# Scores of four node tiles as one level of Strassen's scheme, in a fused graph and attention kernel

## The chip, the cores and the metric

The kernel runs on one core of a Trainium2 chip. The metric is the device time of one execution in microseconds (us); three runs of the kernel before gave a median of 2294.43 us (2293.65 to 2296.58).

The core's engines work in parallel, each on its own queue of instructions and in the order of that queue: TensorE (PE: matmuls, from SBUF into PSUM), VectorE (DVE), ScalarE (ACT), GpSimd (POOL) and SyncE (SP, which here only starts transfers). They wait for one another through semaphores.

## The reference

Inputs are 625 nodes of width 512 with 10,000 edges and the weights of four layers. `x` passes through four residual steps, each on a layer norm of `x`: a hyperbolic graph convolution, a feed-forward step with 8 experts, a plain graph convolution, and an attention over 100 pooled memory slots. Only the last one is touched here. Cut to what matters:

```python
G, H, DQK, DV, L = 8, 16, 128, 128, 100           # 8 groups of 16 heads, 100 slots
q  = (xn @ Wq_w + Wq_b).reshape(b, s, G, H, DQK)   # 625 nodes, 128 heads
kc = einsum('bsd,bsl->bld', k, w).reshape(b, L, G, DQK)   # pooled keys
vc = einsum('bsd,bsl->bld', v, w).reshape(b, L, G, DV)    # pooled values
qk = einsum('bsghd,blgd->bghsl', q, kc) * (1.0 / DQK ** 0.5)
att = softmax(qk, axis=-1)
z  = einsum('bghsl,blgd->bsghd', att, vc).reshape(b, s, G * H * DV)
zn = l2norm(z) * wz_g1
h1 = silu(zn @ wz_w1 + wz_b1)                      # 16384 -> 1024
out = silu((l2norm(h1) * wz_g2) @ wz_w2 + wz_b2)
```

All of it is float32.

## The kernel before

The 625 nodes are five tiles of 125 rows (`P`, `NT`). The attention walks over 32 blocks of four heads (`HB`, `NB`). A block `b` passes through these stages:

- `load(b)` starts the transfers on SyncE's queue: 512 rows of `wz_w1` (2 MB, `wz`), the four heads' columns of `Wq_w` in 16 pieces of 64 KB (`wqraw`), and the bias of the scores, spread over the rows (`cb`). The columns are stored so that 32x32 block transposes complete their turning.
- `turned(b)`: four VectorE transposes, 128x512, from `wqraw` into `wqT` (L1101).
- `folded(b)`: 16 matmuls (`kbps`, L1110) multiply the queries' weights into the pooled keys, so that the queries are never formed; ScalarE copies the result into `keys` (128 x 4 chunks x 400 columns).
- `scores(b)`: for each node tile four matmuls of 400 columns over the four chunks of 128 (`scps`, L1123). VectorE adds the bias while it takes the result out of PSUM (L1124) and finds the maxima (L1126). ScalarE takes exponentials, 20 of 100 columns (L1131), then scales them (L1142).
- `transposes(b, h)` turns a head's attention on TensorE; `value(b, h)` multiplies it with the pooled values (`zps`, L1159). ScalarE squares the result into `zs`, one buffer (L1162), VectorE scales it into `zT` (L1163), and GpSimd adds the squares up in `zsq` (L1166).
- `prepared(b)` forms the sums that two levels of Strassen's scheme need for h1 = z w: `zsums` makes eight sums of values on VectorE (L1173 to L1176), `wsums` four sums of weights on VectorE (`wsum`, and `wz` in place; L1182), and `split` four more on GpSimd for each of the seven outer products (`wq`, eight buffers).
- `hidden(b)`: 98 matmuls of 157 columns (`h1ps`, L1222), gathered six to a PSUM buffer; VectorE adds each buffer into `hacc` (L1234).

PSUM holds four buffers of two banks, which all these stages share in turn (`banks`). `h1ps` of block i-2 is issued at the head of iteration i of the loop (L1239 to L1263); the scores of block i close it, so that TensorE goes from scores straight into `h1ps` of the block before, whose sums `zsums` has just made. Instructions of one engine are placed by a scheduler, which may move them where nothing forbids it; `order(later, sooner)` fixes two of them. `busy` issues matmuls that keep TensorE occupied while it would wait.

Of the kernel before, what the change touches and what calls it, by code (L numbers as in the profile page):

```python
# [28 lines left out]
DC = D // 128  # L29
# [9 lines left out]

QN = 157  # L40

ORDER = (0, 1, 2, 5, 3, 4, 6)


HALF = 375
# [6 lines left out]
AHEAD = 12  # L52

HOT = 8

HB = 4

# [110 lines left out]
def layers_kernel(  # L168
# [885 lines left out]
    with ExitStack() as es:  # L1054
# [14 lines left out]
        zq = [big.tile([128, 7, QN], F32, name=f"zq{i}") for i in range(3)]  # L1069

        NB = G * H // HB
        wz, raw, wqT, keys, cb, att, zquarter, whalf, ready = {}, {}, {}, {}, {}, {}, {}, {}, {}
        heads = ExitStack()
        work = spool(heads, "atwork", 2)
        ps_heads = ExitStack()
# [5 lines left out]
        def load(b):  # L1081


            wz[b] = stream.tile([128, HB, FF2], F32, tag="wz", name="wz", bufs=2)
            nc.sync.dma_start(wz[b], wz_w1[b * HB * DH : (b + 1) * HB * DH, :].rearrange("(c p) m -> p c m", p=128))
            cols = Wq_w[:, b * HB * DH : (b + 1) * HB * DH].rearrange("(i a) (h j b) -> j a h i b", a=32, b=32, j=4)
            raw[b] = []
            for h in range(HB):
                raw[b].append(stream.tile([128, D], F32, tag="raw", name="wqraw", bufs=4))
                to = raw[b][h].rearrange("p (i b) -> p i b", b=32)  # L1090
                for j in range(4):
                    nc.sync.dma_start(to[32 * j : 32 * (j + 1)], cols[j, :, h])
            cb[b] = work.tile([P, HB * L], F32, tag="cb", name="cb", bufs=1)
            nc.sync.dma_start(cb[b], bass.AP(tensor=qbias.tensor, offset=qbias.offset + b * HB * L,
                                             ap=[[0, P], [1, HB * L]]))

        def turned(b):
            wqT[b] = []
            for part in raw[b]:
                wqT[b].append(stream.tile([128, D], F32, tag="wqT", name="wqT", bufs=4))  # L1100
                V.transpose(wqT[b][-1], part)  # L1101

        def folded(b):

            keys[b] = work.tile([128, DC * HB * L], F32, tag="keys", name="keys", bufs=1).rearrange("p (c n) -> p c n", c=DC)
            for c in range(0, DC, 2):
# [4 lines left out]
                                 kcT[:, b * HB // H, :], start=True, stop=True)  # L1111
                A.activation(keys[b][:, c : c + 2, :], ps[:, :, : HB * L], AF.Copy, scale=float(DH) ** -0.5)

        def scores(b):
            s = att[b] = work.tile([128, NT * HB * L], F32, tag="att", name="att", bufs=1)[:P].rearrange("p (t n) -> p t n", t=NT)
            top = rpool.tile([P, NT, HB], F32, tag="a_top", name="a_top")
            tot = rpool.tile([P, NT, HB], F32, tag="a_tot", name="a_tot")
            for t0 in range(0, NT, 2):
                t1 = min(t0 + 2, NT)
                ps = banks("scps")  # L1120
                for t in range(t0, t1):
                    for c in range(DC):
                        T.matmul(ps[:P, t - t0, : HB * L], xnT[:, c, tp(t)], keys[b][:, c, :], start=c == 0, stop=c == DC - 1)  # L1123
                V.tensor_tensor(s[:, t0:t1, :], ps[:P, : t1 - t0, : HB * L],  # L1124
                                cb[b][:, None, :].to_broadcast([P, t1 - t0, HB * L]), op=OP.add)
                V.tensor_reduce(top[:, t0:t1, :].rearrange("p t h -> p (t h)"),  # L1126
                                s[:, t0:t1, :].rearrange("p t (h l) -> p (t h) l", l=L), axis=AX.X, op=OP.max, negate=True)
                for t in range(t0, t1):
                    for h in range(HB):
                        own = s[:, t, h * L : (h + 1) * L]  # L1130
                        A.activation(own, own, AF.Exp, bias=top[:, t, h : h + 1], accum_out=tot[:, t, h : h + 1])  # L1131
            V.reciprocal(tot, tot)  # L1132
            if b == 0:

                sv = s.rearrange("p t (h l) -> p (t h) l", l=L)
                V.tensor_tensor(sv, sv, tot.rearrange("p t h -> p (t h)")[:, :, None].to_broadcast([P, NT * HB, L]),
                                op=OP.mult)
                return
            for t in range(NT):
                for h in range(HB):  # L1140
                    own = s[:, t, h * L : (h + 1) * L]
                    A.activation(own, own, AF.Copy, scale=tot[:, t, h : h + 1])  # L1142
# [12 lines left out]
        def value(b, h):  # L1155
            g = b * HB // H
            ps = banks("zps")
            for u in range(2):
# [3 lines left out]
            A.activation(zs, ps[:, :, : 2 * QN], AF.Square)  # L1162
            scaled = V.tensor_scalar(zT[:, h % 2 : 4 : 2, h // 2, :], ps[:, :, : 2 * QN], g1T[:, b * HB + h : b * HB + h + 1],  # L1163
                                     None, op0=OP.mult)
            if b < NB - 1:
                nc.gpsimd.tensor_tensor(zsq, zsq, zs.rearrange("p u s -> p (u s)"), op=OP.add)  # L1166
                return scaled
            return V.tensor_tensor(zsq, zsq, zs.rearrange("p u s -> p (u s)"), op=OP.add)

        def zsums(z, to):  # L1170


            V.tensor_tensor(to[0], z[1][0], z[1][1], op=OP.add)  # L1173
            V.tensor_tensor(to[1], to[0], z[0][0], op=OP.subtract)
            V.tensor_tensor(to[2], z[0][1], to[1], op=OP.subtract)
            V.tensor_tensor(z[1][0], z[0][0], z[1][0], op=OP.subtract)  # L1176
            return {0: z[0][0], 1: z[0][1], 2: to[2], 5: to[1], 3: z[1][1], 4: to[0], 6: z[1][0]}

        def wsums(engine, w, new, over):

            def combine(x, y, to):
                engine.tensor_tensor(to, x, y, op=OP.subtract)  # L1182
                return to
            t1 = combine(w[0][1], w[0][0], new())
            t2 = combine(w[1][1], t1, new())
# [9 lines left out]
        def prepared(b):  # L1195


            zsums([[zT[:, 2 * u + k] for k in range(2)] for u in range(2)], [zT[:, 4 + i] for i in range(3)])
            z = zT.rearrange("p i k (u s) -> p i k u s", u=2)
            zquarter[b] = zsums([[z[:, :, k, u] for k in range(2)] for u in range(2)], zq)  # L1200
            w = wz[b].rearrange("p (q k) (v m) -> p k v q m", k=2, v=2)
            whalf[b] = wsums(V, [[w[:, k, v] for v in range(2)] for k in range(2)],
                             lambda: work.tile([128, 2, FF2 // 2], F32, tag="wsum", name="wsum", bufs=3), True)
            ready[b] = split(b, ORDER[0])


# [2 lines left out]
        def hidden(b):  # L1209
# [3 lines left out]
            for n, i in enumerate(ORDER):  # L1213
# [3 lines left out]
                for j in ORDER:  # L1217
                    for m in range(2):
# [6 lines left out]
                        if at % 6 == 0 or at == 98:  # L1225
# [3 lines left out]
                            else:  # L1229
                                to = to.rearrange("p (k i) s -> p k (i s)", k=2)  # L1230
                            if b == 0:
                                V.tensor_copy(to, got)
                            else:
                                V.tensor_tensor(to, to, got, op=OP.add)  # L1234


        load(0)
# [1 line left out]
        for i in range(NB + 1):  # L1239
# [10 lines left out]
            if i == 1:  # L1250
                transposes(0, 0)
                transposes(0, 1)
            if i + 1 < NB:
                turned(i + 1)
            if i >= 1:
                for h in range(HB):
                    valued = value(i - 1, h)
# [3 lines left out]
                prepared(i - 1)  # L1261
            if i < NB:
                scores(i)  # L1263


        def combined(p, behind=None):


            for to, x, y in ((1, 1, 0), (3, 3, 0), (0, 3, 5), (6, 6, 3), (2, 2, 0), (5, 5, 6), (4, 4, 6)):
                add = V.tensor_tensor(p(to), p(x), p(y), op=OP.add)  # L1270
                if behind is not None:
                    order(add, behind)
# [96 lines left out]
        R.inverse(rh, rh)  # L1369
        V.tensor_scalar(rh, rh, float(FF2) ** 0.5, None, op0=OP.mult)  # L1370
        for t in range(NT):
            tag = "raw" if t < 4 else "wqT"
            o = stream.tile([128, D], F32, tag=tag, name="o", bufs=4)[:P]
            V.scalar_tensor_tensor(o, outs[t][:P], rh[:, t : t + 1], bz2, op0=OP.mult, op1=OP.add)
            A.activation(o, o, AF.Silu)
            (nc.gpsimd if t % 2 else V).tensor_tensor(o, o, xl[:, t, :], op=OP.add)
# [37 lines left out]
```

## Time and profile before

The profiled execution took 2299.3 us, with a span of 2297.5 us. TensorE's granted clock was 0.989 of full speed on the mean.

| engine | busy us | share of the span |
|---|---|---|
| TensorE, matmuls | 2230.4 | 97% |
| TensorE, weight loads | 1770.4 | 77% |
| VectorE | 1618.5 | 70% |
| GpSimd | 991.4 | 43% |
| ScalarE | 814.8 | 35% |

| stage (us from the span's start) | TensorE | VectorE | ScalarE | GpSimd | granted clock |
|---|---|---|---|---|---|
| first graph convolution and before (0 to 210) | 188.7 | 127.8 | 93.7 | 12.6 | 0.95 |
| experts (210 to 480) | 265.5 | 99.3 | 45.5 | 21.7 | 1.00 |
| attention, 600 us of its steady part (650 to 1250) | 595.9 | 493.1 | 239.5 | 358.5 | 1.00 |
| last values and tail (2180 to 2297) | 90.6 | 66.4 | 27.2 | 27.5 | 0.90 |

The cells of the second table are busy microseconds within the stretch. A profile line of the timeline reads: start (us), duration (us), engine, source line, operation, output<-inputs, shapes, count, and in brackets the idle time before it with what ended it. A line of the chain of waits has start, duration, engine, output and line. A float32 matmul leaves two records, so x40 are 20 matmuls.

### The profile page before, as it was taken

What the parts mean: (1) busy time and instruction counts of PE and PEld (TensorE: products, weight loads), DVE (VectorE), ACT (ScalarE), POOL (GpSimd) and SP (SyncE); (2) the same over time, 40 slices, a digit from 0 to 9 for tenths busy, and PEclk for the clock granted to TensorE, in tenths of its full rate; (3) what the DMA queues carried; (4) which work ended last, traced back from release to release, by engine and by line L of the source; (5) the groups of instructions that cost most, each with busy time, mean ns of one, the idle gap of its engine ahead of it and who ended that gap; (6) DMA issues with size and microseconds to landing.
All of it is one profiled execution on the core that took longest, in us unless ns stands there. A gap on an engine that the chain in (4) does not pass through costs nothing.

```text
span 2297.5 us, 34432 instructions
## 1 busy us (share of the span) xinstructions
PE 2230.4 (97%) x12812; PEld 1770.4 (77%) x12812; DVE 1618.5 (70%) x2303; ACT 814.8 (35%) x2773; POOL 991.4 (43%) x1063
## 2 busy tenths in 40 slices
PE   8999999999999999999999999999999999999987
PEld 5746777756788888888888888888888888888853
DVE  5845333233478888877888887788888778888782
ACT  2354111111333443344344334433443443344322
POOL 1000000100265566656556665555666555566531
PEclk8999999999999999999999999999999999999989
DMA  7002688771222222233222223322222332221110
GB/s 256 8 0 87 233 295 297 237 238 40 36 65 60 59 66 59 60 96 73 59 59 66 59 60 96 73 59 59 66 59 59 96 72 61 59 66 41 42 59 23
DMA packets 326025, 204.68 MB, mean 89 GB/s; under 512 B 275534, under 2 KB 279563, under 8 KB 321000
## 3 DMA queue, kind: packets, MB, share of 16 engines
q1 hardware_dynamic: 317371, 189.65, 28.0%
q10 hardware_dynamic: 3639, 7.56, 0.9%
q0 software_dynamic: 4848, 5.26, 0.9%
q8 instruction: 102, 1.67, 0.3%
q14 instruction: 65, 0.53, 0.1%
HBM read 197.18 MB, written 5.23 MB: 88 GB/s over the span
## 4 chain that ended last, share of the span: by engine, by line
PE 86%; DVE 4%; ACT 4%; POOL 2%; issue 2%; DMA 1%; ACTq 0%; POOLq 0%; DVEq 0%
PE h1ps L1222 35%; PE scps L1123 19%; PE kbps L1110 5%; PE hps L824 5%; PE ops L835 5%; PE zps L1159 3%; POOL zsq L1166 2%; ACT zs L1162 2%; PE stps L918 2%; PE eps L77 2%; PE agps L548 2%; PE atps L1150 2%; PE l1ps L925 1%; DMA b_row<-in_L_gnn_b_dram 1%; DVE hacc L1270 1%
## 5 line engine op out<-in xcount | busy, mean ns | idle before, releaser
L1234 DVE TENSOR_TENSOR hacc<-hacc,h1ps 128x942 f32<-128x942 f32 (+1 forms) x510 | 529.2, 1084 | 11.6 <-PE h1ps L1222 11.6
L1123 PE MATMUL scps<-keys,xnT 128*125 128x400 f32 x1280 | 435.1, 499 | 0.0
L1182 POOL TENSOR_TENSOR wq<-wz 128x256 f32<-128x256 f32 x248 | 241.0, 981 | 405.5 <-PE h1ps L1222 347.3
L1123 PEld LDWEIGHTS scps<-keys,xnT 128*125 128x125 f32 x1280 | 240.0, 188 | 185.1 <-issue 2.6
L1131 ACT ACTIVATE att<-att,a_top 125x100 f32<-125x100 f32 x640 | 231.9, 364 | 361.6 <-DVE a_top L1126 361.6
L1222 PE MATMUL h1ps<-zT,wq 128*128 128x157 f32 x1736 | 302.6, 296 | 0.0
L1222 PE MATMUL h1ps<-zq,wq 128*128 128x157 f32 x1736 | 302.5, 297 | 0.0
L1166 POOL TENSOR_TENSOR zsq<-zsq,zs 128x628 f32<-128x628 f32 x124 | 187.6, 1513 | 201.6 <-ACT zs L1162 201.6
L1222 PEld LDWEIGHTS h1ps<-zT,wq 128*128 128x128 f32 x1736 | 256.2, 189 | 0.0
L1222 PEld LDWEIGHTS h1ps<-zq,wq 128*128 128x128 f32 x1736 | 255.9, 190 | 0.0
L1153 ACT ACTIVATE attT<-atps 100x375 f32<-100x375 f32 (+1 forms) x256 | 92.4, 432 | 397.3 <-PE atps L1150 397.3
L1182 POOL TENSOR_TENSOR wq<-wz,wq 128x256 f32<-128x256 f32 x248 | 210.8, 850 | 19.5
L1163 DVE TENSOR_SCALAR zT<-zps,cols 128x628 f32<-128x628 f32 x128 | 111.6, 872 | 149.0 <-ACT zs L1162 147.6
L1142 ACT ACTIVATE att<-att,a_tot 125x100 f32<-125x100 f32 x620 | 170.2, 365 | 10.7 <-DVE a_tot L1132 10.7
L1159 PE MATMUL zps<-attT,vc 100*128 100x314 f32 x512 | 160.9, 436 | 10.6 <-ACT attT L1153 10.5
L1182 POOL TENSOR_TENSOR wq<-wsum,wq 128x256 f32<-128x256 f32 x186 | 161.5, 868 | 14.7 <-POOL wq L1182 0.3
L1182 POOL TENSOR_TENSOR wq<-wsum 128x256 f32<-128x256 f32 x186 | 135.8, 730 | 65.0 <-PE h1ps L1222 65.0
L1222 PE MATMUL h1ps<-zT,wz 128*128 128x157 f32 x992 | 152.6, 296 | 0.0
L1101 DVE STREAM_TRANSPOSE wqT<-wqraw 128x512 f32<-128x512 f32 x128 | 80.3, 681 | 101.1 <-PE kbps L1110 84.2
L1222 PEld LDWEIGHTS h1ps<-zT,wz 128*128 128x128 f32 x992 | 141.0, 189 | 9.1
L1162 ACT ACTIVATE zs<-zps 128x628 f32<-128x628 f32 x128 | 88.7, 693 | 125.0 <-POOL zsq L1166 111.3
L1159 PEld LDWEIGHTS zps<-attT,vc 100*128 100x128 f32 x512 | 87.4, 191 | 45.9 <-ACT attT L1153 26.9
(408 smaller groups left out, 3438.3 us busy)
## 6 DMA issues: line engine op xcount, KB each, us to landing
w<-in_L_ffn_w_dram SPq DMA_DIRECT2D x16, 4096.0 KB
wz<-in_L_ffn_wz_w_dram SPq DMA_DIRECT2D x32, 2048.0 KB
wqraw<-in_L_ffn_Wq_w_dram SPq DMA_DIRECT2D x512, 64.0 KB
cb<-qbias SPq DMA_DIRECT2D x32, 195.3 KB
wkv<-in_L_ffn_Wkv_w_dram SPq DMA_DIRECT2D x1, 4096.0 KB
W_raw<-in_L_gnn_W_dram SPq DMA_DIRECT2D x2, 1024.0 KB
w<-in_L_ffn_Wkv_w_dram SPq DMA_DIRECT2D x1, 2048.0 KB
l1w<-in_L_gnn_W_dram SPq DMA_DIRECT2D x2, 1024.0 KB
```

The source lines that it names most:

```text
L824: T.matmul(ps[:, i * CAP : (i + 1) * CAP], w1[e][:, c, hc * 128 : (hc + 1) * 128], xgT[e][:, c, :], start=c == 0, stop=c == DC - 1)
L835: T.matmul(ps[:CAP], hT[e][:, hc, :], w2[e][:, hc, :], start=hc == 0, stop=hc == HC - 1)
L1110: folded.last = T.matmul(ps[:, k, h * L : (h + 1) * L], wqT[b][h][:, (c + k) * 128 : (c + k + 1) * 128], kcT[:, b * HB // H, :], start=Tru ...
L1123: T.matmul(ps[:P, t - t0, : HB * L], xnT[:, c, tp(t)], keys[b][:, c, :], start=c == 0, stop=c == DC - 1)
L1131: A.activation(own, own, AF.Exp, bias=top[:, t, h : h + 1], accum_out=tot[:, t, h : h + 1])
L1142: A.activation(own, own, AF.Copy, scale=tot[:, t, h : h + 1])
L1159: T.matmul(ps[:, u, : 2 * QN], vc[:, g * DH : (g + 1) * DH], attT[h % 2][:, 2 * u * QN : 2 * (u + 1) * QN], start=True, stop=True)
L1162: A.activation(zs, ps[:, :, : 2 * QN], AF.Square)
L1166: nc.gpsimd.tensor_tensor(zsq, zsq, zs.rearrange("p u s -> p (u s)"), op=OP.add)
L1182: engine.tensor_tensor(to, x, y, op=OP.subtract)
L1222: T.matmul(ps[:, at % 6 // 3, at % 3 * QN : (at % 3 + 1) * QN], now[j][:, m * 128 : (m + 1) * 128], zquarter[b][j][:, place[i]], start=Tru ...
L1234: V.tensor_tensor(to, to, got, op=OP.add)
```

## The change

For the first four node tiles the scores are a product of a 2x2 block matrix (two halves of the nodes, two halves of the 512-wide contraction) with another (two halves of the contraction, two pairs of heads). In place of eight block products the change forms seven, by one level of Strassen's scheme; the fifth tile is left as it was. The nodes' sums (`xsums`) are made once. The keys' sums are made for each block on GpSimd: two in `folded` (L1121, L1122), with the difference of the two halves of the bias (`dcb`, L1123), and two in `scores` that overwrite parts of `keys` (L1160, L1161). VectorE combines the seven products as it takes them out of PSUM (L1172 to L1178).

The transposes of the queries' weights are done in place, in the buffers into which they are loaded, behind the last eviction of the scores. The weights' sums of `prepared` are placed behind the last `hacc` and behind the scalings of the values. The order of the seven outer products in `hidden` changes, and with it the order of the final sums; three of the five output buffers come from `wqT`, two are new.

The diff, its long parts cut:

```diff
-ORDER = (0, 1, 2, 5, 3, 4, 6)
+ORDER = (0, 1, 3, 4, 5, 6, 2)
...
+PAIR = 2 * L
...
-                raw[b].append(stream.tile([128, D], F32, tag="raw", name="wqraw", bufs=4))
+                raw[b].append(stream.tile([128, D], F32, tag="wqT", name="wqT", bufs=4))
...
         def turned(b):
-            wqT[b] = []
+            wqT[b] = raw[b]
             for part in raw[b]:
-                wqT[b].append(stream.tile([128, D], F32, tag="wqT", name="wqT", bufs=4))
-                V.transpose(wqT[b][-1], part)
+                turn = V.transpose(part, part)
+                if b:
+                    order(turn, scores.last)
...
+            w = [[keys[b][:, 2 * k : 2 * k + 2, v * PAIR : (v + 1) * PAIR] for v in range(2)] for k in range(2)]
+            t1, t2 = (work.tile([128, 2, PAIR], F32, tag=f"kd{i}", name=f"kd{i}", bufs=1) for i in range(2))
+            dcb = work.tile([P, PAIR], F32, tag="dcb", name="dcb", bufs=1)
+            nc.gpsimd.tensor_tensor(t1, w[0][1], w[0][0], op=OP.subtract)
+            nc.gpsimd.tensor_tensor(t2, w[1][1], t1, op=OP.subtract)
+            nc.gpsimd.tensor_tensor(dcb, cb[b][:, PAIR:], cb[b][:, :PAIR], op=OP.subtract)
+            ksum[b] = w, t1, t2, dcb
...
-            for t0 in range(0, NT, 2):
-                t1 = min(t0 + 2, NT)
-                ps = banks("scps")
-                for t in range(t0, t1):
-                    for c in range(DC):
-                        T.matmul(ps[:P, t - t0, : HB * L], xnT[:, c, tp(t)], keys[b][:, c, :], start=c == 0, stop=c == DC - 1)
-                V.tensor_tensor(s[:, t0:t1, :], ps[:P, : t1 - t0, : HB * L],
-                                cb[b][:, None, :].to_broadcast([P, t1 - t0, HB * L]), op=OP.add)
+            def weighed(t0, t1):
...
+            def product(ps, k, z, y):
+                for t in range(2):
+                    for c in range(2):
+                        T.matmul(ps[:P, k, t * PAIR : (t + 1) * PAIR], z[:, c, tp(t)], y[:, c, :], start=c == 0, stop=c == 1)
...
+            first, second, third, fourth = (banks("scps") for _ in range(4))
+            for c in range(DC):
+                T.matmul(first[:P, 0, : HB * L], xnT[:, c, tp(4)], keys[b][:, c, :], start=c == 0, stop=c == DC - 1)
+            plain = V.tensor_tensor(s[:, 4, :], first[:P, 0, : HB * L], cb[b], op=OP.add)
+            if b:
+                order(plain, zsums.last)
+            weighed(4, 5)
+            product(first, 1, xsum[0], w[0][0])
+            product(second, 0, xsum[1], w[1][0])
+            nc.gpsimd.tensor_tensor(w[0][1], w[1][1], w[0][1], op=OP.subtract)
+            nc.gpsimd.tensor_tensor(w[1][0], w[1][0], t2, op=OP.subtract)
+            product(second, 1, xsum[5], t2)
+            product(third, 0, xsum[6], w[0][1])
+            product(third, 1, xsum[4], t1)
+            product(fourth, 0, xsum[2], w[1][1])
+            product(fourth, 1, xsum[3], w[1][0])
...
+            V.tensor_tensor(last, both(first)[:, 1], cb[b][:, None, :PAIR].to_broadcast([P, 2, PAIR]), op=OP.add)
+            V.tensor_tensor(of[:, :, 0:2, :], both(second), last[:, None, :, :].to_broadcast([P, 2, 2, PAIR]), op=OP.add)
+            V.tensor_tensor(of[:, 0, 2:4, :], of[:, 1, 0:2, :], both(third)[:, 0], op=OP.add)
+            V.tensor_tensor(last, both(third)[:, 1], dcb[:, None, :].to_broadcast([P, 2, PAIR]), op=OP.add)
+            V.tensor_tensor(of[:, 1].rearrange("p (a b) n -> p a b n", a=2), mixed,
+                            last[:, None, :, :].to_broadcast([P, 2, 2, PAIR]), op=OP.add)
+            scores.last = V.tensor_tensor(mixed, mixed, both(fourth), op=OP.add)
+            weighed(0, 2)
+            weighed(2, 4)
...
+            behind = iter(hidden.last + scales[b])
             whalf[b] = wsums(V, [[w[:, k, v] for v in range(2)] for k in range(2)],
-                             lambda: work.tile([128, 2, FF2 // 2], F32, tag="wsum", name="wsum", bufs=3), True)
+                             lambda: work.tile([128, 2, FF2 // 2], F32, tag="wsum", name="wsum", bufs=3), True,
+                             lambda op: order(op, next(behind)))
...
+        xsums = big.tile([128, 3, 2, 2 * P], F32, name="xsums")
+        xsum = zsums([[xnT[:, 2 * k : 2 * k + 2, 2 * P * u : 2 * P * (u + 1)] for k in range(2)] for u in range(2)],
+                     [xsums[:, i] for i in range(3)])
...
-            if i + 1 < NB:
-                turned(i + 1)
             if i >= 1:
                 for h in range(HB):
                     valued = value(i - 1, h)
...
             if i < NB:
                 scores(i)
+            if i + 1 < NB:
+                turned(i + 1)
```

Line numbers above L1071 that the prediction gives for new instructions (L1121 to L1178) are those of the changed kernel: L1153 is `plain`, L1172 to L1178 are the six evictions in the order above, L1185 is the scaling of the first block's attention. All others are of the kernel before.

## The prediction

> **What bounds the kernel now.** I read the page's busy shares first, then the chain of waits, then one steady round of the timeline, engine by engine. The shares:
>
> ```profile
> PE 2230.4 (97%) x12812; PEld 1770.4 (77%) x12812; DVE 1618.5 (70%) x2303; ACT 814.8 (35%) x2773; POOL 991.4 (43%) x1063
> ```
>
> TensorE looks like the bound everywhere. But the stage that is changed repeats 31 times, and there the margin of the other engines counts, not their average. The chain of waits over one such round:
>
> ```profile
> 1229.45 3.73 PE kbps L1110 x32
> 1235.13 1.53 POOL zsq L1166
> 1239.13 13.44 PE scps L1123 x40
> 1252.57 26.14 PE h1ps L1222 x196
> 1279.78 3.72 PE kbps L1110 x32
> ```
>
> A round takes 1279.78 - 1229.45 = 50.33 us. From its keys (kbps) to the first hidden product (h1ps) are 23.12 us, of which the scores take 13.44. The step between is paced by zs (ScalarE), zsq (GpSimd), zs, not by TensorE. The same stretch on VectorE:
>
> ```profile
> 1242.04 0.87 DVE L1163 TENSOR_SCALAR zT<-zps,cols 128x628 f32<-128x628 f32 x1 [1.45 <-ACT zs L1162]
> 1242.95 1.32 DVE L1173 TENSOR_TENSOR zT<-zT 128x628 f32<-128x628 f32 x1
> 1244.30 0.81 DVE L1174 TENSOR_TENSOR zT<-zT 128x628 f32<-128x628 f32 x1
> ...
> 1247.82 0.98 DVE L1124 TENSOR_TENSOR att<-scps,cb 125x800 f32<-125x800 f32 x1
> ...
> 1251.14 1.30 DVE L1175 TENSOR_TENSOR zq<-zT,zq 128x1099 f32<-128x1099 f32 x1
> ```
>
> The reader is to see that the eight sums of values (zsums) begin only after the fourth scaling and end at 1252.44, 0.13 us before h1ps starts at 1252.57. So there are two chains of equal length, and shortening the scores alone gains nothing. One eviction (L1124) stands amid the sums, and the first sum takes 1.32 us, its equal-sized neighbours 0.81.
>
> Why 1.32: a sum that reads two SBUF tiles does not run beside a GpSimd sum.
>
> ```profile
> 1219.49 1.21 DVE L1182 TENSOR_TENSOR wsum<-wz,wsum 128x1024 f32<-128x1024 f32 x1
> 1219.52 1.77 POOL L1182 TENSOR_TENSOR wq<-wz 128x256 f32<-128x256 f32 x1
> ```
>
> This GpSimd sum usually takes 0.73; here it lasts until just after VectorE's. Of two that ask, the earlier goes first, the other waits for all of it. A wsum alone then takes about 1.09 (1.34 when asked 0.25 before GpSimd was free, at 1216.14).
>
> **The change part by part**, laid over this round with its keys at 1229.45.
>
> *Fewer products.* Scores: 40 records are 20 matmuls of 400 columns in 13.44, 0.672 each, 1.68 ns a column; h1ps (98 of 157 columns in 26.14, 0.267 each) has the same rate. Four tiles cost 16 x 0.672 = 10.75; seven products of 4 matmuls of 200 columns cost 28 x 0.336 = 9.41. TensorE is spared 1.34 a round, 43 in 32.
>
> *New order of waits.* The built program's order of instructions shows: L1153 (eviction of the fifth tile) follows the last zsums on VectorE, by an explicit order. The product of keys' first quarter (into the second half of that same PSUM tile) is placed last of the seven and waits for L1153. The first h1ps waits for L1172, the eviction of that product, since the scores hold all four PSUM buffers. So the old chain gets a tail: L1153 0.56 (565 ns for 125x400), product 4 x 0.336 plus 0.05, L1172 0.56, with three hand-overs of 0.05 together 2.66. Queued behind L1153 on VectorE is every other eviction; behind the seventh product is all of h1ps.
>
> *Weights' sums.* They leave h1ps (four of 1.2, where VectorE had room) and go: one after the last hacc, two between scalings, one (wz) after the fourth, ahead of zsums. Laid out with the exclusive turns: zsq0 1235.15 to 1236.66, wsum2 to 1237.77, zsq1 to 1239.28, wsum3 to 1240.38, zsq2 to 1241.89, zs3 and the fourth scaling to 1243.52 (now 1242.91). wz then waits for zsq3 to 1244.21 and ends 1245.30. The first wsum is free: the keys' sums after it on GpSimd wait for ScalarE's keys anyway.
>
> *Keys' sums on GpSimd.* A 128x256 sum takes 0.73, 128x628 1.51; so 128x400 is 1.03. Two (L1121, L1122) fit before zsq0: keys are there at 1232.27 and 1234.06, they end at 1235.13. L1160, L1161 stand behind zsq3, where wz has asked first: L1160 runs 1245.30 to 1246.33, and the first of zsums waits for it; L1161 goes between zsums 1 and 2 (1247.10 to 1248.13). TensorE waits 1.9 for L1160, which is hidden, for the seventh product is later. The rest of zsums (7 at today's spacing, 7.26) ends at 1255.39. With the tail h1ps starts at 1258.05: **5.48 later than 1252.57**. Without any GpSimd conflict it would be 1242.91 + 1.09 + 7.9 + 2.66 = 1254.56, 2.0 later: the floor.
>
> *Evictions and transposes in h1ps.* After its start VectorE has L1173 (0.98), L1174, L1175 (0.56 each), hacc, L1176 (about 0.95, as 628 elements take 0.81), hacc, L1178 (0.98), a transpose (0.62), two reduces (0.90 each), two transposes, and only then the third hacc, done 10.9 us after the start; the seventh h1ps buffer needs it at 6 x 1.60 = 9.6. **1.35 a round**. Thereafter hacc (1.05) catches up with TensorE (1.60 per buffer).
>
> *Clock.* TensorE idles 4.15 us (1251.80 to 1255.95) ahead of the seventh product. The nearest row:
>
> ```profile
> 2235.65 4.02 PE L1325 MATMUL h1ps<-zT,wz 128*128 128x314 f32 x8 [3.99 <-DVE hacc L1327]
> 2250.82 2.11 PE h1ps L1325 x8
> ```
>
> After 3.99 idle the same eight records take 4.02 instead of 2.11; and at 563.0 to 566.0 TensorE was only 58% busy, never idle for long, and the granted clock was 0.50 thereafter. The Trainium skill (TensorE: Matmul & The Clock Gate, "What's actually happening") has it that the clock halves after a whole idle window of about 3.4 us, with windows that run free. By that, an idle 4.15 holds a whole window in 22% of rounds: 0.22 x 1.9 = 0.4 a round. By the rows it falls nearly always: 1.35 to 1.9. Since part of a slow start is absorbed in the 1.35 above, I take 1.0.
>
> *At nothing.* SP: the 16 weight loads of a block wait for kbps in place of the old transposes (both near 3.7 us after kbps starts), and cb is now behind all of them (before, three were behind it); they are read some 30 us later. The wz load goes out 2 us later (both last groups read wz); it too has over 40 us. cb waits for L1172; dcb on GpSimd, with two wq sums of the fifth group behind it, comes 10 us after that. ScalarE's last 16 exps start 8 us into h1ps rather than 0.8, the 20 scalings end near 20; transposes come at 27. If these covers go, each late microsecond is one of the round. The order of products and of `combined` changes no count; the tail's output buffers have no wait.
>
> *First block, once.* Its evictions, 16 exps (0.36 each), L1185 (2.25) and the last transpose now follow the last product, with kbps of block 1 behind that transpose. I get the first attention transposes at 639.7 instead of 627.83: +12.
>
> **Sum.** 31 x (5.48 + 1.35 + 1.0) + 12 = 255. The profiled execution took 2299.3 (span 2297.5 and 1.8 around it), 4.9 above the median 2294.43; on the median 255 gives 2549. Within the case, with the clock at 0 to 1.9: 2518 to 2577.
>
> **The rivals.**
> - *No contention.* GpSimd slips into gaps: 2.0 + 1.35 + 0.3 a round, 125, so 2419. Against: 1.77 and 1.32 above.
> - *VectorE keeps its turn* and L1160 runs only after zsums: then five products of 1.35 follow it, about 9.0 + 1.35 + 1.9 = 12.25 a round, 392, so 2686. Against: the earlier asker went first at 1219.5.
> - *The other side: TensorE stays the bound.* If evictions go ahead of zsums, as L1124 does at 1247.82, the seventh product waits for nothing and the gain of 1.34 x 31 less 12 comes through: 2265. It decides if the tail's 2.66 and wz's 1.09 fall out of the chain, so that h1ps starts before 1252.57. Against: the order is written out, and holds in all 31 rounds of the built program.
>
> **How the numbers follow.** Main case 0.70; no contention 0.12; kept turn 0.12; other side 0.04; a cancelling sum within 0.2% (4.6 us, what a measurement here can tell from no change) 0.02. Faster 0.04, same 0.02, slower 0.94. The range, from the floor case's 2420 to 2640 towards the kept turn, leaves out about 0.2.
>
> **What would show it.** Right: a round of near 58 us; DVE wz after the fourth scaling, zsums ending near 26 us after kbps; TensorE idle about 4 us before the last scps product (released by L1153), then a short wait for L1172; a wait near the seventh h1ps buffer; clock below 1.0 in these rounds. Wrong: zsq and wsum running at once; h1ps beginning less than 23 us after kbps; any wait on a DMA.

## The result, and the profile after

The changed kernel takes 2579.93 us (median of 4 runs, 2573.37 to 2586.27) against 2295.07 us of the kernel before in the same comparison (4 runs): a ratio of 1.124, 95% interval 1.121 to 1.127. It is slower by 285 us; 2549 was forecast. The profiled execution has a span of 2577.9 us. The busy shares of its page:

```profile
PE 2296.8 (89%) x13580; PEld 1949.7 (76%) x13580; DVE 1802.4 (70%) x2435; ACT 819.3 (32%) x2773; POOL 1103.1 (43%) x1223
```

TensorE is busy 66 us longer although it has 43 us less to do: some of its work was clocked slower. And it waits: 281 us of the span are idle, where there were 67. The chain of waits through one round (start, length, what) shows where:

```profile
1402.12 3.56 PE kbps L1114 x32
...
1414.87 0.87 DVE zT L1212
1415.74 1.77 DVE wz L1223
1417.52 1.56 DVE zT L1285
1419.11 1.52 DVE zT L1286
...
1425.88 1.30 DVE zq L1287
1427.18 0.49 DVE att L1153
1427.72 2.88 PE scps L1145 x8
1430.62 0.59 DVE att L1172
...
1441.15 1.03 DVE hacc L1280
1442.23 16.85 PE h1ps L1268 x124
1459.08 1.07 PE atps L1199 x10
1460.14 3.57 PE kbps L1114 x32
```

Read it downwards: fourth scaling, wz, sums of values (the first two twice as long as they should be), the fifth tile's eviction L1153, the seventh product, its eviction L1172, then h1ps, which stops once more for a hacc. The seventh product takes 2.88 us where the products before it start 1.35 apart. The reason is in the timeline by windows (the window, its length, busy time and number of instructions of PE, PEld, DVE, ACT and POOL, then the granted clock, the DMA share and GB/s), here for this round's seventh product and for the same place in a long round:

```profile
1428.00:1431.00 3.00, 2.58 (x8) 2.03 (x7) 0.65 (x2) 1.55 (x8) 0.00 (x0) 0.50 0.00 0
...
2012.00:2016.00 4.00, 3.07 (x9) 2.53 (x9) 1.41 (x4) 1.55 (x8) 0.00 (x0) 0.50 0.00 0
2016.00:2020.00 4.00, 4.00 (x15) 4.00 (x16) 2.48 (x4) 0.00 (x0) 0.45 (x1) 0.50 0.15 50
2020.00:2024.00 4.00, 4.00 (x24) 4.00 (x24) 3.21 (x4) 0.00 (x0) 3.16 (x4) 0.77 0.00 0
```

TensorE had been idle for 3.58 us, as in every round, and got half its clock (0.50); in no round does the seventh product take less than 2.5 us. In the first round that lasted some 3 us, in the other it went on into h1ps to about 2022 (0.77 is the mean of the last window). So there are rounds of 58.0 us and rounds of up to 60.3. The waits between 700 and 2400 us (in total, times, longest):

```profile
PE scps L1145 <- DVE att L1153: 103.9, 29, 3.6
PE scps L1145 <- POOL keys L1160: 40.1, 29, 1.4
PE h1ps L1268 <- DVE hacc L1280: 23.4, 29, 1.1
PE h1ps L1268 <- DVE att L1172: 19.3, 29, 0.7
```

All four were named in the prediction. No wait of TensorE on a transfer is among the waits of these rounds.

### The profile page after: what moved, and what is told of

Same layout as the page of the kernel before. It is cut to its first block, busy times and chain, and to the rows that moved or that the text cites. A ratio compares the mean times of both kernels' runs of the same rounds, so it can differ in the third digit from the quotient of the medians.

```text
span 2577.9 us, 36300 instructions
## 1 busy us (share of the span) xinstructions
PE 2296.8 (89%) x13580; PEld 1949.7 (76%) x13580; DVE 1802.4 (70%) x2435; ACT 819.3 (32%) x2773; POOL 1103.1 (43%) x1223
## 4 chain that ended last, share of the span: by engine, by line
PE 52%; DVE 27%; POOL 7%; issue 7%; ACT 5%; DMA 1%; DVEq 0%; POOLq 0%; ACTq 0%
PE h1ps L1268 24%; POOL zsq L1216 6%; PE hps L826 5%; PE kbps L1114 4%; PE ops L837 4%; PE scps L1145 4%; ACT zs L1211 3%; DVE wz L1223 2%; DVE hacc L1280 2%; DVE zT L1285 2%; DVE zT L1286 2%; PE stps L920 2%; DVE zq L1285 2%; DVE zq L1286 2%; DVE zq L1287 2%
## 5 line engine op out<-in xcount | busy, mean ns | idle before, releaser
L1145 PE MATMUL scps<-keys,xnT 128*125 128x200 f32 x1024 | 240.8, 387 | 155.0 <-DVE att L1153 112.2
L1145 PEld LDWEIGHTS scps<-keys,xnT 128*125 128x125 f32 x1024 | 205.5, 217 | 184.0 <-DVE att L1153 121.8
L1268 PE MATMUL h1ps<-zq,wq 128*128 128x157 f32 x1736 | 285.9, 307 | 25.1 <-DVE hacc L1280 23.4
L1268 PEld LDWEIGHTS h1ps<-zT,wq 128*128 128x128 f32 x1736 | 266.4, 196 | 0.0
L1223 POOL TENSOR_TENSOR wq<-wz 128x256 f32<-128x256 f32 x248 | 182.2, 735 | 153.9 <-PE h1ps L1268 97.4
L1268 PE MATMUL h1ps<-zT,wz 128*128 128x157 f32 x992 | 173.8, 323 | 20.7 <-DVE att L1172 20.7
L1223 POOL TENSOR_TENSOR wq<-wz,wq 128x256 f32<-128x256 f32 x248 | 182.5, 736 | 19.6 <-POOL wq L1223 0.3
L1268 PEld LDWEIGHTS h1ps<-zT,wz 128*128 128x128 f32 x992 | 154.1, 207 | 37.3 <-DVE att L1172 37.3
L1208 PE MATMUL zps<-attT,vc 100*128 100x314 f32 x512 | 160.9, 436 | 12.3 <-ACT attT L1202 12.2
L1114 PE MATMUL kbps<-kcT,wqT 128*128 128x100 f32 x1024 | 122.6, 279 | 9.0 <-DVE wqT L1103 7.3
L1114 PEld LDWEIGHTS kbps<-kcT,wqT 128*128 128x128 f32 x1024 | 119.8, 196 | 9.9 <-DVE wqT L1103 7.7
```

Source lines behind the costliest of these rows:

```text
L1114: folded.last = T.matmul(ps[:, k, h * L : (h + 1) * L], wqT[b][h][:, (c + k) * 128 : (c + k + 1) * 128], kcT[:, b * HB // H, :], start=Tru ...
L1145: T.matmul(ps[:P, k, t * PAIR : (t + 1) * PAIR], z[:, c, tp(t)], y[:, c, :], start=c == 0, stop=c == 1)
L1208: T.matmul(ps[:, u, : 2 * QN], vc[:, g * DH : (g + 1) * DH], attT[h % 2][:, 2 * u * QN : 2 * (u + 1) * QN], start=True, stop=True)
L1223: op = engine.tensor_tensor(to, x, y, op=OP.subtract)
L1268: T.matmul(ps[:, at % 6 // 3, at % 3 * QN : (at % 3 + 1) * QN], now[j][:, m * 128 : (m + 1) * 128], zquarter[b][j][:, place[i]], start=Tru ...
```

## The experiments

The size of the loss was close to the forecast, so the question was which of its parts are real, and whether anything else is in it. Theory: the tail behind the sums of values, the exclusive turns of VectorE and GpSimd, the place of the transposes and the halved clock, each a part of its own. Rivals: that contention alone is the cost; that the clock alone is; that h1ps has too little of VectorE wherever things stand. All kernels start from the changed one, except two that start from the kernel before. Their line numbers differ by some lines. The rounds, worked out from the starts of kbps and of the first h1ps in each trace (means over 29 or 30 rounds, us):

| kernel | time, median | ratio to before, 95% | kbps to first h1ps | whole round |
|---|---|---|---|---|
| before | 2295 to 2298 | 1 | 23.03 | 50.32 |
| changed | 2579.93 | 1.121 to 1.127 | 29.35 | 59.05 |
| fifth eviction free | 2478.38 | 1.077 to 1.081 | 27.19 | 55.72 |
| weights' sums free | 2512.60 | 1.093 to 1.097 | 27.19 | 56.67 |
| TensorE kept warm | 2529.67 | 1.100 to 1.104 | 28.05 | 57.30 |
| before, weights' sums moved | 2333.09 | 1.015 to 1.018 | 22.94 | 51.46 |
| late transposes | 2543.93 | 1.105 to 1.109 | 28.83 | 57.77 |
| no third and fourth keys' sum | 2499.18 | 1.086 to 1.089 | 26.84 | 56.50 |
| all places changed | 2354.86 | 1.023 to 1.026 | 23.24 | 51.54 |
| and two square buffers | 2311.87 | 1.004 to 1.007 | 21.57 | 50.27 |
| and h1ps's start cleared | 2270.18 | 0.987 to 0.991 | 21.20 | 49.03 |
| before, two square buffers | 2276.36 | 0.989 to 0.993 | 22.43 | 49.71 |

**The fifth tile's eviction set free.**

```diff
-            if b:
-
-                order(plain, zsums.last)
```

> The changed kernel without the explicit order of the fifth tile's eviction behind the last sum of values: that eviction then stands behind the first sum of values and the eviction of the seventh product behind the first of the last four sums; the sums of weights stay between the values. If the tail of waits behind the sums (2.66 us as predicted; 4.1 us as traced, with the seventh product at half clock) is one of the two costs, h1ps starts some 2.6 us earlier after its keys (26.5 us instead of 29.1; the two evictions and a reduce, 1.6 us together, now lie amid the sums), so about 31 x 2.6 = 80 us: 2500 us, and the sums of values end last ahead of h1ps. If the sharing [...]between VectorE and GpSimd is the whole cost: 2560 to 2580. If TensorE becomes the bound (the case of the other side that was forecast): 2265.

Measured: 2478.38 us, 102 less, and h1ps 2.2 us earlier. The tail is gone, so contention alone is not the cost. But the sums of values do not end last. TensorE's timeline of one round:

```profile
1375.50 1.52 PE L1145 MATMUL scps<-keys,xnT 128*125 128x200 f32 x8
1376.85 0.84 PE L1145 MATMUL scps<-kd,xsums 128*125 128x200 f32 x4
1380.90 2.66 PE L1145 MATMUL scps<-keys,xnT 128*125 128x200 f32 x8 [3.21 <-DVE att L1153]
1383.36 1.52 PE L1145 MATMUL scps<-kd,xsums 128*125 128x200 f32 x4
```

The scheduler, left free, put the product that shares a PSUM tile with the fifth tile ahead of four others. It waits 3.2 us for L1153 (the eviction still stands behind wz and the first sum), and what is queued behind it on TensorE waits with it; the clock behind the wait is halved here too (0.55 on the mean from 1381 to 1384 us). The gain was larger than expected, 102 for 80, and the mechanism partly another one.

**The weights' sums set free.**

```diff
-                             lambda: work.tile([128, 2, FF2 // 2], F32, tag="wsum", name="wsum", bufs=3), True,
-                             lambda op: order(op, next(behind)))
+                             lambda: work.tile([128, 2, FF2 // 2], F32, tag="wsum", name="wsum", bufs=3), True)
```

> The changed kernel with the four sums of weights not held between the values: three stand among the hacc sums of h1ps, the fourth after the last hacc and ahead of the first scaling. If the exclusive turns of these sums with the squares' sums (zsq) are a cost of their own, the fourth scaling comes 0.6 us earlier and the sums of values 2.5 us earlier; h1ps starts at about 26.6 us after its keys instead of 29.1, with the tail of waits still behind it: 2500 us. If only the tail counts, since the sums of weights use idle time of VectorE: 2570 to 2590. If VectorE in h1ps has no room for three more sums of 1.2 us: h1ps is stalled further and it is slower than 2590.

Measured: 2512.60 us, 67 less, h1ps 2.2 us earlier. The place of these sums is a cost of its own, and VectorE has room for them in h1ps, where the kernel before had them. The sums of values begin 1.8 us earlier and end 1.3 earlier, less than the 2.5 expected. The run does not separate the turn from the work: wz itself (1.1 us without a wait) and its wait for the fourth zsq (0.7) leave the chain together. Most of the other 0.9 us goes with the clock, which is halved in 18 of 29 rounds here and in all 29 of the changed kernel.

**TensorE kept warm.**

```diff
...
-            product(first, 1, xsum[0], w[0][0])
...
-            product(fourth, 1, xsum[3], w[1][0])
+            warm = product(fourth, 1, xsum[3], w[1][0])
+            for _ in range(14 if b else 0):
+                mm = T.matmul(fourth[:, 1, 2 * PAIR : 512], full, full[:, : 512 - 2 * PAIR], start=True, stop=True)
+                order(mm, warm)
+                warm = mm
+            product(first, 1, xsum[0], w[0][0], warm)
```

> The changed kernel with 14 matmuls of 112 columns (about 0.19 us each, 2.6 us) that compute nothing wanted, placed on TensorE between the sixth and the seventh product, where it was idle for 3.6 us. All waits of VectorE and GpSimd stay; one more transpose stands ahead of the third hacc (0.6 us). If the idle time halves the clock and that is a cost beside the waits: the seventh product takes 1.4 instead of 2.9 us, h1ps starts at full clock, the long rounds (59.3 to 60.5 us) go, and a round takes 2 to 2.5 us less, minus up to 0.6: 2510 to 2540. If the clock is no cost of its own (half clock is absorbed by the waits in h1ps): 2570 to 2590. If it is the main cost of the change: below 2450.

Measured: 2529.67 us, 50 less, and every round the same (57.29 to 57.32). The timeline, and the window around the seventh product:

```profile
1348.22 3.27 PE L1170 MATMUL scps<-full 128*128 128x112 f32 x28
1351.97 1.62 PE L1145 MATMUL scps<-keys,xnT 128*125 128x200 f32 x8 [0.47 <-DVE att L1156]
...
1365.80 0.40 PE L1275 MATMUL h1ps<-zq,wq 128*128 128x157 f32 x1 [1.67 <-DVE hacc L1287]
```

```profile
1350.00:1353.00 3.00, 2.53 (x20) 2.35 (x19) 2.48 (x4) 0.45 (x3) 0.00 (x0) 1.00 0.00 0
```

The seventh product takes 1.62 us again and the clock is 1.00, with all waits of VectorE and GpSimd in place. 3 us of work that nobody wants on the busiest engine make the kernel 2% faster. In h1ps the third hacc is later by the transpose that moved ahead of it: the stall is 1.67 instead of 1.08 us. So the clock was worth 59.05 - 57.30 = 1.75 us a round net, and 2.3 with those 0.6 added back.

**The kernel before, with the weights' sums moved.**

```diff
...
+            behind = iter(hidden.last + scales[b])
             whalf[b] = wsums(V, [[w[:, k, v] for v in range(2)] for k in range(2)],
-                             lambda: work.tile([128, 2, FF2 // 2], F32, tag="wsum", name="wsum", bufs=3), True)
+                             lambda: work.tile([128, 2, FF2 // 2], F32, tag="wsum", name="wsum", bufs=3), True,
+                             lambda op: order(op, next(behind)))
...
```

> The kernel before, with nothing changed but the place of the four sums of weights: one after the last hacc, two between scalings, the fourth after the last scaling, as in the changed kernel; no Strassen, no keys' sums. If the exclusive turns with the squares' sums cost by themselves: the sums of values begin 2.35 us later and end about 2.8 us later (one more reduce falls among them), h1ps waits for them alone, 31 x 2.8 = 87: about 2382 us, up to 2440 if TensorE's idle time ahead of h1ps also halves its clock. If VectorE has room there and the turns are free: 2290 to 2300, or less, since h1ps is relieved of four sums.

Measured: 2333.09 us, 1.14 us a round, less than half of what was expected. VectorE and TensorE of one round:

```profile
1354.78 1.84 DVE L1183 TENSOR_TENSOR wz<-wz 128x1024 f32<-128x1024 f32 x1
1356.54 0.80 DVE L1174 TENSOR_TENSOR zT<-zT 128x628 f32<-128x628 f32 x1
```

```profile
1364.07 1.23 PE L1227 MATMUL h1ps<-zT,wz 128*128 128x157 f32 x8
1366.34 0.80 PE L1227 MATMUL h1ps<-zq,wz 128*128 128x157 f32 x4 [1.04 <-DVE zq L1176]
```

wz waits for the fourth zsq and takes 1.84, as in the changed kernel, and the sums are late. But the first eight records of h1ps (1.1 us) need only the first sums and run before the last sum is done: the sums end 2.1 us later, and that absorbs 1.0 of it. In the changed kernel the sums are followed by L1153, the product and L1172, which the very first h1ps waits for, so that there nothing is absorbed. The same delay costs more with the tail behind it.

**Late transposes.**

```diff
...
+                            if at == 18 and b + 1 < NB:
+                                for op in scores.tops:
+                                    order(op, hidden.last[0])
+                            if at in (24, 30, 36, 42) and b + 2 < NB:
+                                part = raw[b + 2][at // 6 - 4]
+                                order(V.transpose(part, part), hidden.last[0])
...
```

> The changed kernel with the four transposes of the queries' weights put one each behind the fourth, fifth, sixth and seventh hacc of h1ps, and the two reduces of the other scores behind the third hacc; nothing else is moved. If the stall of h1ps (1.08 us a round as traced) comes from the transposes and reduces ahead of the third hacc: that hacc ends 7.5 us after the start of h1ps, the stall goes, h1ps takes 27.2 to 27.8 us, and the total is 31 x 1.1 = 34 us less: 2545. If h1ps is bound by VectorE's whole work in it and not by that place: 2575 to 2585. The waits ahead of h1ps stay.

Measured: 2543.93 us, 36 less, where 34 were worked out. In the waits between 700 and 2400 us only one of the two lines for h1ps is left:

```profile
PE h1ps L1269 <- DVE att L1172: 19.3, 29, 0.7
```

The stall belongs to the place, not to the amount of VectorE's work.

**Without the third and fourth sum of keys.**

```diff
-            nc.gpsimd.tensor_tensor(w[0][1], w[1][1], w[0][1], op=OP.subtract)
-            nc.gpsimd.tensor_tensor(w[1][0], w[1][0], t2, op=OP.subtract)
```

> The changed kernel without the third and fourth sum of keys on GpSimd (the two products that need them are made with the keys' quarters as they are, so those scores are not the reference's). If these two sums alternate with the first two sums of values, each turn costing VectorE the length of a GpSimd sum: the sums of values end 2.0 us earlier a round, TensorE has no wait for them, and h1ps starts 2.0 us earlier behind the same tail: about 2515 us. If the fourth square's sum, not the keys', is what VectorE waits for: 2570 to 2580.

Measured: 2499.18 us, 81 less. The first sums of values, on VectorE:

```profile
1331.60 0.80 DVE L1283 TENSOR_TENSOR zT<-zT 128x628 f32<-128x628 f32 x1
1332.43 0.81 DVE L1284 TENSOR_TENSOR zT<-zT 128x628 f32<-128x628 f32 x1
```

In the changed kernel, with GpSimd's two sums of keys beside them:

```profile
1417.44 1.63 DVE L1285 TENSOR_TENSOR zT<-zT 128x628 f32<-128x628 f32 x1
1419.11 1.52 DVE L1286 TENSOR_TENSOR zT<-zT 128x628 f32<-128x628 f32 x1
1416.40 2.01 POOL L1160 TENSOR_TENSOR keys<-keys 128x400 f32<-128x400 f32 x1
1418.37 1.60 POOL L1161 TENSOR_TENSOR keys<-keys,kd 128x400 f32<-128x400 f32 x1
```

That is the alternation with L1160 and L1161. From the start of the fourth scaling to the end of the sums are 10.67 us instead of 12.31: 1.64 for two turns, where 2.0 was expected. The turns are 31 x 1.64 = 51 us; the other 30 us of the gain go with TensorE's clock. Ahead of the seventh product TensorE is idle for 3.67 us in every round, longer than in the changed kernel, and yet the clock is halved in only 16 of 29 rounds. In one round that product takes 2.00 us (from 1340.33), in the next 1.62 (from 1397.73). The shortest stretch of half clock in these traces is 3.41 us, all others in the rounds two or three times that, so these are windows of that length, laid where the clock changes; the last number but two is the clock:

```profile
1338.02:1341.44 3.42, 1.11 (x6) 1.11 (x7) 2.83 (x4) 0.52 (x3) 0.00 (x0) 1.00 0.00 0
1341.44:1344.85 3.41, 2.74 (x11) 2.21 (x10) 2.41 (x4) 1.03 (x6) 0.00 (x0) 0.50 0.09 34
...
1392.64:1396.05 3.41, 1.42 (x9) 1.11 (x7) 3.38 (x4) 0.00 (x0) 0.00 (x0) 1.00 0.00 0
1396.05:1399.46 3.41, 1.62 (x8) 1.31 (x8) 2.27 (x4) 1.14 (x7) 0.00 (x0) 1.00 0.00 0
1399.46:1402.87 3.41, 2.85 (x21) 2.85 (x22) 3.34 (x5) 0.41 (x3) 0.82 (x2) 1.00 0.17 59
```

In the first round the idle time leaves TensorE 1.11 us of work in one window, and the next is at half clock. In the other round it falls across two windows, with 1.42 and 1.62 us of work, and the clock stays whole.

**All places changed at once.** The fifth eviction ahead of the sums, the seventh product fifth of the seven, its eviction ahead of the last sum, the weights' sums late in h1ps and ahead of the first scaling, the transposes as above:

```diff
...
+            if b:
+                order(zsums.ops[0], plain)
...
+            mm = product(third, 1, xsum[4], t1)
+            mm = product(first, 1, xsum[0], w[0][0], mm)
+            mm = product(fourth, 0, xsum[2], w[1][1], mm)
+            product(fourth, 1, xsum[3], w[1][0], mm)
...
+            if b:
+                order(zsums.ops[6], freed)
...
-                             lambda op: order(op, next(behind)))
+                             lambda op: order(scales[b][0], op))
...
```

> The changed kernel with its order of work changed in all places at once, nothing computed differently: the fifth tile's eviction right behind the fourth scaling, the seventh product as fifth of the seven on TensorE, its eviction ahead of the last sum of values; two sums of weights late in h1ps and two between the last hacc and the first scaling; reduces behind the third hacc, transposes one each behind the fourth to seventh. If the tail, the turns of the weights' sums and the transposes' place are together the cost: the sums of values end 24.5 us after the keys (the two evictions, a reduce and the turns with the keys' sums still lie among them), h1ps starts at once and takes 27.2 us, a round 51.8: 2355 us, up to 2400 if TensorE's idle time of some 2.7 us still halves the clock. If TensorE becomes the bound: 2265. If something that was not named remains: over 2420.

Measured: 2354.86 us. 225 of the 285 us are gone with nothing computed otherwise, so nothing unnamed of that size is left. The parts tried alone add up to more than the loss (102 + 67 + 50 + 36 + 81 = 336): most of them also lessen the half clock, which is counted several times. By an estimate (half of TensorE's busy time at half clock) it costs 2.7 us a round in the changed kernel, 2.0 with the fifth eviction free, 1.1 with the weights' sums free, 1.8 without the keys' sums, and nothing with TensorE kept warm.

**Two buffers for the squares besides.**

```diff
...
-                         lambda: work.tile([128, FF2 // 4], F32, tag="wq", name="wq", bufs=8), False)
+                         lambda: work.tile([128, FF2 // 4], F32, tag="wq", name="wq", bufs=6), False)
...
-            zs = work.tile([128, 2, 2 * QN], F32, tag="zs", name="zs", bufs=1)
+            zs = work.tile([128, 2, 2 * QN], F32, tag="zs", name="zs", bufs=2)
```

> As the kernel with all places changed at once, and besides: two buffers for the squares (zs), so that ScalarE need not wait for GpSimd's sum of the one before (two of the eight quarter buffers wq make the room), and the fifth tile's eviction behind the first sum of values. If the step zs, zsq, zs ahead of the fourth scaling is what remains: the fourth scaling ends 11.7 instead of 13.5 us after the keys, the sums of values at about 22.2 to 23.0, TensorE's products at 21.9; a round takes 49.4 to 50.2 us: 2280 to 2305, beside the 2295 of the kernel before. If the turns of GpSimd and VectorE only move (four squares' sums, two keys' sums and the quarter sum that now comes late, all against eight sums of values): the sums still end at 24 to 25 us and it is 2340 to 2370.

Measured: 2311.87 us, 7 above the range of the first theory. The sums were in time (first h1ps 21.57 us after kbps), but three small stalls came in h1ps instead:

```profile
1316.88 1.33 PE L1272 MATMUL h1ps<-zT,wz 128*128 128x157 f32 x8 [0.23 <-DVE att L1174]
...
1318.99 1.33 PE L1272 MATMUL h1ps<-zq,wq 128*128 128x157 f32 x8 [0.24 <-DVE att L1177]
...
1322.63 0.77 PE L1272 MATMUL h1ps<-zT,wq 128*128 128x157 f32 x4 [0.18 <-DVE hacc L1284]
```

**And the start of h1ps cleared.** The evictions L1174 and L1177 one sum earlier each, the first hacc ahead of the long add, the fifth tile's reduce later, transposes behind the sixth to ninth hacc; in the first block the transposes ahead of the division:

```diff
...
-                order(zsums.ops[6], freed)
+                order(zsums.ops[7], freed)
...
+                order(zsums.ops[6], freed)
...
+                            if at == 6 and b + 1 < NB:
+                                order(scores.mid, hidden.last[0])
+                            if at == 12 and b + 1 < NB:
+                                order(scores.last, hidden.last[0])
...
+                if b:
+                    order(scores.divided, turn)
...
```

> As the kernel with two buffers for the squares, with the small stalls of TensorE at the start of h1ps taken away (0.5 for the first buffer, 0.4 for the second, 0.35 for the fourth, about 1.0 to 1.3 us a round in that trace, at a granted clock of 1.00): the seventh product's eviction stands ahead of the last but one sum of values and the next eviction ahead of the last; the fifth tile's reduce goes behind the fifth hacc; the first hacc stands ahead of the long add in the scores, the other reduces behind the fourth hacc, the transposes behind the sixth to ninth; in the first block the transposes of the next weights stand ahead of the division of the attention. If TensorE is the bound of the round once these are gone: 49.0 to 49.3 us a round, 31 x 1.0 to 1.3 less, and 5 us less at the first block: 2265 to 2280, faster than the kernel before by 0.8 to 1.4%. If VectorE, now full from the sums of values to the ninth hacc, only moves the stall: 2300 to 2315.

Measured: 2270.18 us (2269.02 to 2273.83), 1.1% faster than the kernel before (0.9 to 1.3%). One whole round:

```profile
1226.21:1275.20 48.99, 48.68 (x329) 45.77 (x329) 45.38 (x49) 19.99 (x75) 34.21 (x38) 1.00 0.28 69
```

TensorE is busy for 48.68 of 48.99 us at full clock; it is the bound.

**The kernel before with two buffers for the squares**, the same two lines as above:

> The kernel before with nothing but two buffers for the squares and six for the quarter sums. Its fourth scaling then ends 1.75 us earlier and so do the sums of values; but its scores end 0.1 us ahead of h1ps, so if there are two chains of equal length, shortening one alone gains 0.1 us a round: 2290 to 2298, no difference. If the sums of values are the only chain: 31 x 1.75 = 54 less, 2242. If six quarter buffers are too few: slower than 2300.

Measured: 2276.36 us (2273.74 to 2277.57), 0.9% faster. This was wrong in all three cases: 0.61 us a round came, where 0.1 was expected. Two lines of TensorE tell why, first the kernel before, then this one:

```profile
1288.12 1.33 PE L1159 MATMUL zps<-attT,vc 100*128 100x314 f32 x4 [0.34 <-ACT attT L1153]
```

```profile
1326.44 2.29 PE L1159 MATMUL zps<-attT,vc 100*128 100x314 f32 x8
```

The copy attT of the fourth head stood behind a square on ScalarE that waited for GpSimd's zsq. TensorE waited for the copy, and all later products with it. With a second buffer the square does not wait, and the last two products of values run in one go. From the third product's start to the scores are 2.73 us before and 2.12 now, which is all of the 0.61. A round then has TensorE at work without a gap (49.71 us).

So most of what the best version gains over the kernel before comes with two lines that have nothing to do with Strassen's scheme. Its own share is the difference to this last kernel: 0.7 us a round, less some 14 us once in the first block. By the medians that is 6 us; the two intervals of the ratio (0.987 to 0.991, 0.989 to 0.993) overlap, so that a gain of the scheme itself is not established.

## Why the prediction was right, and where it was off

- **The sign and the mechanism** were right: the order written out by hand makes a tail of L1153, product and L1172, and all the named waits were there in all rounds read. Taking the written order away alone gave 102 us back. That the number came so close is in part luck: two errors of opposite sign, worked out below.
- **The weights' sums and the turns.** Forecast: wz waits for the fourth zsq, L1160 and L1161 alternate with the first sums. The trace has just that (wz, then two sums of 1.56 and 1.52). The sums of values end 25.06 us after kbps instead of 25.94: the fourth scaling ended 13.6 rather than 14.1 us after kbps, and a turn of a keys' sum cost 0.82 (1.64 for two), not 1.03.
- **h1ps 5.48 later.** Measured are 29.35 - 23.03 = 6.3. The 5.48 was free of the clock. With TensorE kept warm it is 28.05 - 23.03 = 5.0, less than forecast since the sums are 0.9 early; the rest, 1.3, is the seventh product at half clock. TensorE was idle for 3.58 us ahead of it, not for 4.15.
- **The seventh buffer, 1.35.** Up to 1.08 in the trace, 0.8 on the mean, since in the long rounds TensorE is slow itself; the transposes put elsewhere gave 36 us, 1.16 a round.
- **The clock, 1.0: this term was mis-sized.** By the rows it was 1.35 to 1.9 (1.7, if the later row is read in the timeline too, where it lasts 2.28), by the rule of the Trainium skill (TensorE: Matmul & The Clock Gate, "What's actually happening"), a whole idle window of about 3.4 us, 0.4; the value taken lay between. With TensorE kept warm it proved to be 1.75 net and 2.3 in full. The upper end by the rows was too low, since in the long rounds the half clock reaches into h1ps. Windows of 3.41 us are in the traces, but the one before the fall need not be wholly idle. In the rounds of the five kernels whose clock is halved there (the changed one, fifth eviction free, weights' sums free, late transposes, no keys' sums) the clock fell 119 times, each time behind a window with TensorE busy for at most 41% of it, and never behind the 2117 windows at full clock with more. So the idle time alone does not decide, but where it lies in the windows: 3.58 us halved the clock in all 29 rounds of the changed kernel, 3.67 us without the keys' sums in 16 of 29. Nor could the chance of 22% be taken for each round anew: rounds of 58.03 us are 17 windows of 3.413, so such a round meets the windows where the last one did. For other stages the 41% is no rule: the prediction's own row from 563 us was 58% busy and was followed by half clock.
- **The balance of a round.** Without the clock 5.48 + 1.35 = 6.83 was forecast, and 57.30 - 0.6 - 50.32 = 6.4 came (the 0.6 is the transpose moved by the warm products). With the clock it is 8.73, where 7.83 was forecast: the waits were put 0.4 too high, the clock 1.3 too low (1.0 for 2.3). The difference makes 31 x (8.73 - 7.83) = 28 of the 31 us missed.
- **The first block, 12.** Its first attention transposes came 36.4 us after kbps instead of 24.1: 12.3.
- **"Two chains of equal length, and shortening the scores alone gains nothing"** was only half true. The scores did end with the sums, but TensorE had lost 0.6 us before them through a wait on ScalarE, which the same step zs, zsq, zs caused. The prediction named that step as what paces the sums, and did not see that it also holds TensorE. This has no part in the 285 us.
- **The rivals.** No contention and the kept turn fell with the two sums at 1.56 and 1.52 us. The other side, TensorE as the bound at 2265, needed more than the evictions ahead of the sums: with those and the weights' sums out of the way it was 2355, and it came (2270) only with the second square buffer and the start of h1ps cleared as well. That 2270 is near 2265 is luck: 20 of the 26 us gained come with the second square buffer, which the forecast of 2265 did not have.

## What to carry to other kernels

A saving on the bound engine is worth nothing if it hangs a serial tail (eviction, product, eviction) behind the chain that ends last; ask first which instruction releases the next stage, and put what it needs ahead of work that can be late. Moving work into another engine's idle gaps isn't free where the sums of the two engines take turns, as here: the gap has to be free on both. And look at single-buffered tiles that tie two engines into lockstep: a second buffer, paid for with slack elsewhere, was worth 20 us here, and the whole scheme put in order 6 more, which is not established.

## What the runs showed of the hardware that was not expected

- 3.58 us without a product halved TensorE's clock in every round, and the half clock lasted for one, two or three windows of 3.41 us, so equal rounds took 58.0 to 60.3 us; what sets that number is not shown. A longer idle time, 3.67 us, halved it in about half of the rounds of another kernel: behind a window with TensorE busy for 0.28 to 0.41 of it, not behind two with 0.42 to 0.47 each. 14 idle products (2.6 us of work by estimate, 3.3 as traced) in that gap made the rounds equal within 0.03 us.
- A VectorE sum of two SBUF tiles that met a GpSimd sum took 0.75 us longer (128x628: 0.80 alone, about 1.55 against a keys' sum), and both records show the wait as busy time (the keys' sum 2.01 instead of 1.03). An idle column says nothing of it; the mean of a group beside that of its undisturbed neighbours does.
